# A graph-attention layer: the first difference of W_v by an adding transfer, query loads on GpSimd, and other tiles turned by VectorE

## The chip, the cores and the metric

The kernel runs on one core of a Trainium2 chip. The metric is the device time of one execution in microseconds (us). The engines are named as the profile names them: PE is TensorE, DVE is VectorE, ACT is ScalarE, POOL is GpSimd, SP is SyncE. Each has one instruction queue that it works off in order. PE's weight loads (PEld) run beside its matmuls. Transfers are issued by SP, ACT or POOL and carried out by sixteen DMA engines.

## The reference

One layer over 2708 nodes with 1024 features, all in float32:

```python
h = jnp.maximum(_layernorm(x, axis=-1), 0.0)
q = h @ W_q.T + b_q
k = h @ W_k.T + b_k
v = h @ W_v.T + b_v
z = scale * (q @ k.T)
spare_z = z * adj_tensor
spare_z = jnp.where(spare_z == 0.0, -10000.0, spare_z)
attn = jax.nn.softmax(spare_z, axis=1)
return x + jax.nn.relu(attn @ v)
```

The adjacency matrix is random with about 0.15% ones, some four per row.

## The kernel before

**What is computed.** W_q and W_k are folded into one matrix M, so that a score is the product of a row of q = h M + b with a row of h. Since a row has few neighbours, no 2708 x 2708 product is formed: the rows are sorted by degree into 22 tiles of 128 rows (P), and for each tile and each neighbour slot POOL gathers the neighbours' rows of h by an indirect transfer (`gather`, L610). DVE multiplies a gathered tile g with the tile's queries pq and sums along the row (L863, one score for each row), and after the softmax adds the gathered tiles up with their weights into u (L923, L929 for a half tile). The output is relu(u W_v + b) + x.

**The two large products.** Both h M and u W_v are done for pairs of tiles in a Strassen-Winograd scheme: seven products of blocks in place of eight. Its sums of blocks of the weights are T0 = W01 − W00, T1 = W11 − T0, T2 = W11 − W01 and T3 = W10 − T1 (subtractions in L1270 on DVE, in `T`, which the profile calls `wlow`); its sums of blocks of the rows are named s1 to s4 (`blocks`, L711 to L742, DVE). There are 20 units: 0 to 9 make q for a pair of tiles, 10 to 19 make the output of the pairs (6,5), (4,3), (2,0), (20,7), (17,13), (18,12), (19,11), (15,10), (14,1) and (16,9). Tile 8 has no partner: it comes alone, in four plain products behind unit 19 (L1372 to L1380). One product is four matmul instructions of 128x512 over 128x128 (L1011, eight rows of the profile). In PE's queue the seven of a unit stand so: s2, a12, s4, s3, then two of the next unit (a11, s1, issued by `opened`), then a22.

**Order.** The places between a unit's products are numbered: `after(i)` with i from 0 to 6 is called behind each, and the code there says what is issued at (unit, i). DVE's queue is in the order in which the program names its instructions. Those of PE, ACT, POOL and SP are placed by a scheduler as their inputs become ready in its model. The attention is a stream of steps, advanced by `advance` by a share of time at each `after`, over tiles in the order 6, 5, 4, 3, 2, 21, 0, 20, 7, 17, 13, 18, 12, 19, 11, 15, 10, 14, 1, 16, 9, 8. Tile 21 is a second half for rows of high degree. `fill` issues gathers as slots come free: `free` holds the slots, and pieces of the weight buffers join it once their weights are used. `fetch` gets a tile's queries pq: tiles 0 to 7 by a POOL gather, the others from `q_late` by a plain SP load (L833; L831 for the half tile 21). There are two pq buffers.

**Turning u.** A product needs u with features on the partitions. Three ways are used. A *faced* tile goes through DRAM: ACT copies it permuted (L945) and stores it (L947), SP loads it in four pieces (`by_quarters`, L700), and DVE turns it in 32x32 blocks (`faces`, L705, STREAM_TRANSPOSE). Any other tile is turned by PE, in eight matmuls with the identity (`half_turned`, L415), and ACT copies from PSUM (L718). A tile whose unit is near (`near`) is held in SBUF for it, without the trip. L940 decides which tiles are faced, by the place `now` at which the tile is done. Before, these are all tiles of the first five output units, and tile 8, whose rows are loaded at the end of unit 18 and turned by DVE behind the first product of unit 19 (`T_alone`). PE turns 18, 12, 19, 11, 15, 10, 14, 1, 16 and 9.

**The weights.** M's place is taken by W_v block by block as M's last products are done (L1263 to L1266, SP). W01 comes first, asked for at 219.26 us into M[:, 0, 1], which the products of M do not read. T0 is made at (9, 2).

Of the kernel before, what the change touches and what calls it, by code (L numbers as in the profile page):

```python
# [18 lines left out]
P = 128  # L19
# [46 lines left out]
def tile_preln_masked_attention(  # L66
# [753 lines left out]
    def fetch(t):  # L820

        if t not in g_of:
            ask(t)
        if t == BARE:
            return
        assert formed.issuperset(range(EARLY) if t < EARLY or t == SECOND else (t,)), t
        tq[t] = work.tile([P, D], FT, tag="hT", name=f"pq_{t}", bufs=2)
        if t == SECOND:
            assert EARLY in formed
            gather(tq[t][:HP], q_dram[:, :], t, SLOTS - WIDE, HP)  # L830
            nc.sync.dma_start(tq[t][HP:], q_late[:HP, :])  # L831
        elif t >= EARLY:
            nc.sync.dma_start(tq[t], q_late[(t - EARLY) * P:(t - EARLY + 1) * P, :])  # L833
        else:
            got = gather(tq[t], q_dram[:, :], t, SLOTS, P)
            if t == order[0]:
                first_q.append(got)
# [81 lines left out]
    def sums(t):  # L919
# [19 lines left out]
        unit = next((n for n, pair in enumerate(units) if pair[0] == "o" and t in pair[1:]), len(units))  # L939
        if now < [unit - 2, 2] and unit <= len(q_pairs) + 4 or unit >= len(units) - 1:  # L940
            faced_tiles.add(t)
# [74 lines left out]
    def opened(n):  # L1016
# [7 lines left out]
        nc.scalar.copy(Y, X)  # L1024
        products.append(add_block(Z, ops["s1"], T[:, 0]))
        p5 = small("p5")
# [203 lines left out]
    for n, unit in enumerate(units):  # L1230
# [13 lines left out]
        def after(i):  # L1244
# [13 lines left out]
            if n == FIRST and i in (1, 4, 5):  # L1258
                for g in slots[:4] if i == 1 else slots[4:6] if i == 4 else slots[6:8]:
                    with tc.issue_after(sorted_at[-1].ins):  # L1260
                        nc.vector.memset(g, 0.0)
            b11, b12, b21, b22 = M[:, 0, 0], M[:, 0, 1], M[:, 1, 0], M[:, 1, 1]
            for at, place, src in (((-1, 0), b12, of_wv(0, 1)), ((0, 0), b11, of_wv(0, 0)), ((0, 2), T[:, 1], of_wv(1, 1)),  # L1263
                                   ((0, 3), b21, of_wv(1, 0)), ((0, 4), b22, of_wv(1, 1))):
                if (n - last_q, i) == at:
                    nc.sync.dma_start(place, src)  # L1266
            for at, place, a, b in (((0, 2), T[:, 0], b12, b11), ((0, 4), T[:, 1], T[:, 1], T[:, 0]),
                                    ((1, 0), T[:, 2], b22, b12), ((1, 1), T[:, 3], b21, T[:, 1])):
                if (n - last_q, i) == at:
                    nc.vector.tensor_sub(place, a, b)  # L1270
            if (n - last_q, i) == (1, 1):
                free.extend(M.rearrange("p i j (a c) w -> p i j a (c w)", a=2)[:, 0, 1, a, :] for a in range(2))
            if (n, i) == (FIRST, 5):
# [11 lines left out]
            if nxt is not None:  # L1285
# [12 lines left out]
                if i == 6 and n + 2 < FIRST:  # L1298
                    natural_rows(n + 2)
                if i == (2 if n in (FIRST, last_q) else 4) and n + 2 > FIRST and n + 2 < len(units) and n + 2 not in rows_of:  # L1300
                    while units[n + 2][0] == "o" and not done.issuperset(units[n + 2][1:]):
# [13 lines left out]
            if nxt is None and i == 1:  # L1315
                uT = work.tile([P, D], FT, tag="hT", name="T_alone", bufs=2).rearrange("p (c q) -> p c q", q=P)
                faces(uT, single["rows"], 0, DC)
                single["turned"] = uT
            if n == len(units) - 2 and i == 6:
                while alone not in done:  # L1320
                    advance(1.0)
                single["rows"], = load_rows(("o", alone))
            if nxt is None and i == 3:
# [48 lines left out]
    uT, (X, Z), p1 = single["turned"], single["banks"], single["first"]  # L1372
    add_block(Z, uT[:, 0:4, :], T[:, 0])
    add_block(Z, uT[:, 4:8, :], M[:, 1, 1])
# [188 lines left out]
```

## Time and profile before

| | us |
|---|---|
| three runs | 637.52, 638.18, 638.37; median 638.18 |
| the profiled execution | 638.0, of which its span 636.3 |
| granted clock of PE, mean | 0.995 |
| PE busy | 624.6 |
| DVE busy | 525.7 |
| POOL busy | 361.8 |
| ACT busy | 283.5 |

Up to about 120 us the kernel folds the matrices and reads the adjacency matrix; the q units follow, and the output units from about 390 us on. Behind the last matmul there are some 9 us of the last DVE sum, its POOL scatter and the transfer. In the lines quoted below, a timeline's row has the start, the duration, the engine, the line of the kernel, the operation, output<-input, and in brackets how long the engine was idle before it and what it waited for. A row of groups ends with busy time and mean duration in ns. A row of the waits has the engine and its tile or line, what it waited for, then us in total, times and the longest. A row of the windows has the length, then busy time and instructions of PE, PEld, DVE, ACT and POOL, the granted clock, the share of the DMA engines and GB/s.

### The profile page before, as it was taken

The page shows a single profiled execution, that of the slowest core. Times are in us where ns is not written, and L with a number is a line of the kernel's source. Part 1 is how long each engine was busy: PE and PEld are TensorE (multiplying, and loading weights), DVE is VectorE, ACT ScalarE, POOL GpSimd, SP SyncE. Part 2 cuts the span into 40 slices and gives each one's busy share as a digit, 9 for nine tenths or more (in the row PEclk, how much of TensorE's full clock was granted, in tenths as well). Part 3 has the DMA queues.
Part 4 walks back from the last instruction along what each step waited for, and adds up shares of the span by engine and source line. Part 5 has one row for each costly group of instructions (what it writes and reads, how often), then busy time and mean ns, then how long its engine had stood idle before and what let it go on. Part 6 is the DMA issues. An engine that isn't in the chain of part 4 may idle for free.

```text
span 636.3 us, 6139 instructions
## 1 busy us (share of the span) xinstructions
PE 624.6 (98%) x1627; PEld 315.5 (50%) x1627; DVE 525.7 (83%) x1021; ACT 283.5 (45%) x421; POOL 361.8 (57%) x383
## 2 busy tenths in 40 slices
PE   9999999999999999999999999999999999999994
PEld 5777766444444544444444434444444444444441
DVE  5999889897995755997889999999999989898341
ACT  3539975859667533424341243443343333422300
POOL 2649960975868277563742563576566777632431
PEclk9999999999999999999999999999999999999997
DMA  8998897598696439986699998999999999893761
GB/s 339 407 372 310 334 351 298 199 342 328 246 382 221 170 113 334 326 299 196 194 289 323 297 412 216 311 318 324 351 378 321 334 299 295 242 289 95 210 217 40
DMA packets 62352, 180.11 MB, mean 283 GB/s; under 512 B 10039, under 2 KB 17031, under 8 KB 61672
## 3 DMA queue, kind: packets, MB, share of 16 engines
q0 software_dynamic: 25136, 78.41, 39.4%
q1 hardware_dynamic: 31242, 80.19, 35.8%
q10 hardware_dynamic: 5934, 21.06, 8.5%
q8 instruction: 15, 0.25, 0.2%
q14 instruction: 25, 0.20, 0.1%
HBM read 147.23 MB, written 42.31 MB: 298 GB/s over the span
## 4 chain that ended last, share of the span: by engine, by line
PE 85%; DVE 6%; issue 4%; DMA 3%; SPq 1%; POOL 0%; ACT 0%; POOLq 0%; DVEq 0%; ACTq 0%
PE ps L1011 38%; PE psy L1011 28%; PE ps_y L476 6%; PE ps_x L476 4%; PE ps_z L476 4%; PE pt L415 3%; DVE u L923 2%; DMA g<-h_dram,tab 1%; DMA or<-u_dram 1%; DVE junk L863 1%; DVE s L722 1%; DVE wlow L1270 1%; PE ps_y L511 1%; SPq L700 1%; DVE q L1092 0%
## 5 line engine op out<-in xcount | busy, mean ns | idle before, releaser
L610 POOL DMA_INDIRECT g<-h_dram,tab x94 | 121.4, 1291 | 84.4 <-DVE u L923 31.1
L1011 PE MATMUL ps<-M,a 128*128 128x512 f32 x320 | 144.0, 593 | 0.0
L1011 PE MATMUL psy<-wlow,s 128*128 128x512 f32 x320 | 143.9, 592 | 0.0
L863 DVE SCALAR_TENSOR_TENSOR junk<-g,pq 128x1024 uint8<-128x1024 f32 x93 | 113.7, 1222 | 14.0 <-DMA g<-h_dram,tab 10.9
L1011 PEld LDWEIGHTS ps<-M,a 128*128 128x128 f32 x320 | 59.8, 190 | 70.8 <-issue 70.6
L1011 PEld LDWEIGHTS psy<-wlow,s 128*128 128x128 f32 x320 | 59.7, 190 | 70.2 <-issue 69.4
L923 DVE SCALAR_TENSOR_TENSOR u<-g,coef,u 128x1024 f32<-128x1024 f32 x69 | 88.4, 1281 | 6.9 <-ACT u L912 5.8
L389 DVE FIND_INDEX8 at<-ones,adj 128x8 uint32<-128x685 f32 (+1 forms) x88 | 74.5, 865 | 0.0
L1011 PE MATMUL psy<-wlow,a 128*128 128x512 f32 x160 | 72.0, 593 | 1.4 <-DVE q L1092 1.4
L1011 PE MATMUL ps<-M,s 128*128 128x512 f32 x160 | 72.1, 592 | 0.0
L1011 PE MATMUL ps<-wlow,s 128*128 128x512 f32 x160 | 72.0, 593 | 0.1
L368 ACT ACTIVATE sized<-adj 128x2708 uint8<-128x2708 f32 (+1 forms) x22 | 54.3, 2468 | 7.5 <-DMA adj<-in_adj_dram 6.2
L298 POOL TENSOR_TENSOR hsum<-hsum,x 128x256 f32<-128x256 f32 (+1 forms) x56 | 38.7, 729 | 25.6 <-DVE wlow L444 21.2
L1110 POOL DMA_INDIRECT y<-in_x_dram,tab x19 | 34.8, 1832 | 29.1 <-ACT y L1127 15.9
L1011 PEld LDWEIGHTS psy<-wlow,a 128*128 128x128 f32 x160 | 30.3, 190 | 40.0 <-issue 37.1
L1011 PEld LDWEIGHTS ps<-wlow,s 128*128 128x128 f32 x160 | 30.3, 190 | 38.6 <-issue 37.9
L1011 PEld LDWEIGHTS ps<-M,s 128*128 128x128 f32 x160 | 30.3, 190 | 38.1 <-issue 37.4
L912 ACT ACTIVATE u<-g,coef 128x1024 f32<-128x1024 f32 x18 | 20.7, 1147 | 32.1 <-DVE coef L911 32.1
L808 POOL DMA_INDIRECT out_dram<-y,tab x21 | 25.0, 1188 | 16.4 <-DVE flag L1354 6.1
L626 POOL DMA_INDIRECT tab_dram<-tab,pos_i x22 | 21.9, 995 | 20.7 <-DVE pos_i L689 15.3
L276 ACT ACTIVATE x<-x,r 128x1024 f32<-128x1024 f32 (+1 forms) x22 | 25.9, 1235 | 7.3 <-POOL r L266 7.3
L760 ACT COPY ps<-bp_sb 128x512 f32<-128x512 f32 x42 | 24.5, 595 | 7.2 <-DVE y L1145 6.7
(251 smaller groups left out, 843.5 us busy)
## 6 DMA issues: line engine op xcount, KB each, us to landing
adj<-in_adj_dram SPq DMA_DIRECT2D x21, 1354.0 KB, 11.3
x<-in_x_dram SPq DMA_DIRECT2D x21, 512.0 KB, 3.9
h_dram<-x ACTq DMA_DIRECT2D x21, 512.0 KB, 8.7
u_dram<-v ACTq DMA_DIRECT2D x13, 512.0 KB, 6.4
or<-u_dram SPq DMA_DIRECT2D x52, 128.0 KB, 7.0
q_late<-q SPq DMA_DIRECT2D x12, 512.0 KB, 6.0
pq<-q_late SPq DMA_DIRECT2D x12, 512.0 KB, 8.6
M<-in_wv_dram SPq DMA_DIRECT2D x4, 1024.0 KB
```

The lines of the kernel that those rows point to most:

```text
L276: nc.scalar.activation(xs[i][:n], xs[i][:n], AF.Relu, bias=r[:n, 4, i:i + 1], scale=r[:n, 3, i:i + 1])
L298: small.append(nc.gpsimd.tensor_add(hsum[:n, cols], hsum[:n, cols], xt[:n, cols]))
L368: nc.scalar.activation(sized[:n], a[:n, :, :PW], AF.Abs, accum_out=total[:n, t:t + 1])
L389: nc.vector.max_index(at[:n, k - first_k, g, :], ones[:n, 0:8], a[:n, g, :])
L476: mm = nc.tensor.matmul(bank, a_tile(o + H * a[0], a[1], i), b(o), start=first and o == 0, stop=(o == H - 1), skip_group_check=True)
L610: return nc.gpsimd.indirect_dma_start(out=dst, out_offset=None, in_=src, in_offset=off, bounds_check=N - 1, oob_is_err=False)
L760: nc.scalar.copy(return_[h], row[:, h * NB:(h + 1) * NB])
L808: to = nc.gpsimd.indirect_dma_start(out=out, out_offset=bass.IndirectOffsetOnAxis(ap=ptab.bitcast(U32)[:n, t, SLOTS:SLOTS + 1], axis=0), i ...
L863: chained(lambda: nc.vector.scalar_tensor_tensor(junk, g_of[t][s], 1.0, tq[t], op0=ALU.mult, op1=ALU.mult, accum_out=zall[:, t, s:s + 1]))
L923: chained(lambda: nc.vector.scalar_tensor_tensor(u, g_of[t][s], coef[:, s:s + 1], u, op0=ALU.mult, op1=ALU.add))
L1011: mm = nc.tensor.matmul(bank, a[:, c, :], b[:, c, :], start=False, stop=(c == 3), skip_group_check=True)
L1110: return nc.gpsimd.indirect_dma_start(out=y[:n], out_offset=None, in_=x, in_offset=off, compute_op=ALU.add)
```

## The change

- **First difference.** W00 is loaded into M[:, 0, 1], at SP's place where W01 was loaded before. ACT scales it by −1 in place in two instructions, and a POOL transfer with `accum_op=add` adds W01 from DRAM to it: T0 stands there without DVE. T0's subtraction goes; T2 is now formed as T1 − W00. The s1 products of the output units and of tile 8 read M[:, 0, 1], and T[:, 0] joins the gather slots at (9, 0), where two pieces of M[:, 0, 1] joined at (10, 1) before.
- **Queries.** The twelve L833 loads and L831 go from SP's queue to POOL's.
- **Faced tiles.** By the new condition 18, 12 and 19 are faced. Tile 8 no longer is: it is held, turned by PE ahead of unit 19's s2 product, and copied by ACT. Tile 15 is now held too.
- **Rows sooner.** From unit 9 on the rows of unit n + 2 are loaded at i = 2 and not at i = 4 where both tiles are done.

```diff
@@ fetch
             gather(tq[t][:HP], q_dram[:, :], t, SLOTS - WIDE, HP)
-            nc.sync.dma_start(tq[t][HP:], q_late[:HP, :])
+            nc.gpsimd.dma_start(tq[t][HP:], q_late[:HP, :])
         elif t >= EARLY:
-            nc.sync.dma_start(tq[t], q_late[(t - EARLY) * P:(t - EARLY + 1) * P, :])
+            nc.gpsimd.dma_start(tq[t], q_late[(t - EARLY) * P:(t - EARLY + 1) * P, :])
@@ sums
-        if now < [unit - 2, 2] and unit <= len(q_pairs) + 4 or unit >= len(units) - 1:
+        if now < [unit - 2, 1] and unit <= len(q_pairs) + 6 or unit == len(units) - 1:
             faced_tiles.add(t)
@@ opened
-        products.append(add_block(Z, ops["s1"], T[:, 0]))
+        products.append(add_block(Z, ops["s1"], T[:, 0] if units[n][0] == "q" else M[:, 0, 1]))
@@ after
-            b11, b12, b21, b22 = M[:, 0, 0], M[:, 0, 1], M[:, 1, 0], M[:, 1, 1]
-            for at, place, src in (((-1, 0), b12, of_wv(0, 1)), ((0, 0), b11, of_wv(0, 0)), ((0, 2), T[:, 1], of_wv(1, 1)),
+            b11, t1, b21, b22 = M[:, 0, 0], M[:, 0, 1], M[:, 1, 0], M[:, 1, 1]
+            for at, place, src in (((-2, 0), t1, of_wv(0, 0)), ((0, 0), b11, of_wv(0, 0)), ((0, 2), T[:, 1], of_wv(1, 1)),
                                    ((0, 3), b21, of_wv(1, 0)), ((0, 4), b22, of_wv(1, 1))):
                 if (n - last_q, i) == at:
                     nc.sync.dma_start(place, src)
-            for at, place, a, b in (((0, 2), T[:, 0], b12, b11), ((0, 4), T[:, 1], T[:, 1], T[:, 0]),
-                                    ((1, 0), T[:, 2], b22, b12), ((1, 1), T[:, 3], b21, T[:, 1])):
+            if (n - last_q, i) == (-2, 6):
+                for h in range(2):
+                    nc.scalar.activation(t1[:, 2 * h:2 * h + 2], t1[:, 2 * h:2 * h + 2], AF.Copy, scale=-1.0)
+                nc.gpsimd.dma_start(t1, of_wv(0, 1), accum_op=ALU.add)
+            for at, place, a, b in (((0, 4), T[:, 1], T[:, 1], t1), ((1, 0), T[:, 2], T[:, 1], b11),
+                                    ((1, 1), T[:, 3], b21, T[:, 1])):
                 if (n - last_q, i) == at:
                     nc.vector.tensor_sub(place, a, b)
-            if (n - last_q, i) == (1, 1):
-                free.extend(M.rearrange("p i j (a c) w -> p i j a (c w)", a=2)[:, 0, 1, a, :] for a in range(2))
+            if (n - last_q, i) == (0, 0):
+                free.extend(T.rearrange("p k (a c) w -> p k a (c w)", a=2)[:, 0, a, :] for a in range(2))
...
-                if i == (2 if n in (FIRST, last_q) else 4) and n + 2 > FIRST and n + 2 < len(units) and n + 2 not in rows_of:
+                ready = n >= last_q and n + 2 < len(units) and done.issuperset(units[n + 2][1:])
+                if (i == 4 or i == 2 and (n == FIRST or ready)) and n + 2 > FIRST and n + 2 < len(units) and n + 2 not in rows_of:
...
             if nxt is None and i == 1:
-                uT = work.tile([P, D], FT, tag="hT", name="T_alone", bufs=2).rearrange("p (c q) -> p c q", q=P)
-                faces(uT, single["rows"], 0, DC)
-                single["turned"] = uT
-            if n == len(units) - 2 and i == 6:
                 while alone not in done:
                     advance(1.0)
-                single["rows"], = load_rows(("o", alone))
+                r, = load_rows(("o", alone))
+                single["turned"] = turned(r, "alone")
@@ behind the units
-    add_block(Z, uT[:, 0:4, :], T[:, 0])
+    add_block(Z, uT[:, 0:4, :], M[:, 0, 1])
```

The change moves instructions at three places. The first is DVE's queue in unit 9, where `q` is the last pair's queries, `or` a faced tile's rows and `s`, `a` its blocks. Before:

```order
L1329 TENSOR_TENSOR bp_sb<-bp_sb 128x512
L1270 TENSOR_TENSOR wlow<-M 128x2048
L923 SCALAR_TENSOR_TENSOR u_2292<-g_1412,coef,u_2292 128x1024
L705 STREAM_TRANSPOSE a_2319<-or_2235 128x4x4x32
L705 STREAM_TRANSPOSE s_2321<-or_2235 128x4x4x32
...
L1095 TENSOR_TENSOR q_2272<-ps_2218,u_2314 128x512
L1270 TENSOR_TENSOR wlow<-wlow 128x2048
```

and now:

```order
L1331 TENSOR_TENSOR bp_sb<-bp_sb 128x512
L923 SCALAR_TENSOR_TENSOR u_2295<-g_1412,coef,u_2295 128x1024
L705 STREAM_TRANSPOSE a_2321<-or_2238 128x4x4x32
L705 STREAM_TRANSPOSE s_2323<-or_2238 128x4x4x32
...
L1095 TENSOR_TENSOR q_2275<-ps_2221,u_2317 128x512
L1274 TENSOR_TENSOR wlow<-wlow,M 128x2048
```

T0's subtraction is gone from between the bias and the weighted sum; T1's (now L1274) stays, and reads M[:, 0, 1].

The second is POOL's queue in the middle of the output units: `g`, `M` and `wlow` are gather slots, `y` the rows of x that are added, `out_dram` the scatter of a finished tile. Before:

```order
L1110 DMA y_2706<-in_x_dram,tab 128x1024
L808 DMA out_dram<-y_2562,tab 2708x1024
L610 DMA g_1403<-h_dram,tab 128x1024
L610 DMA g_1404<-h_dram,tab 128x1024
L610 DMA g_1405<-h_dram,tab 128x1024
L1110 DMA y_2841<-in_x_dram,tab 128x1024
L808 DMA out_dram<-y_2705,tab 2708x1024
L610 DMA g_1406<-h_dram,tab 128x1024
```

and now, with the names numbered by tile:

```order
L1110 DMA y_0_2708<-in_x_dram,tab_97 128x1024
L808 DMA out_0_dram<-y_3_2564,tab_97 2708x1024
L833 DMA pq_10_2977<-q_late_65 128x1024
L610 DMA g9_1412<-h_dram_63,tab_97 128x1024
L610 DMA g10_1413<-h_dram_63,tab_97 128x1024
L610 DMA g0_1403<-h_dram_63,tab_97 128x1024
L1110 DMA y_20_2847<-in_x_dram,tab_97 128x1024
L808 DMA out_0_dram<-y_2_2707,tab_97 2708x1024
L833 DMA pq_14_3082<-q_late_65 128x1024
L610 DMA g1_1404<-h_dram_63,tab_97 128x1024
```

A plain load of queries now stands ahead of the gathers, once for each tile. Likewise the half tile's load and the adding transfer have come into POOL's queue; the latter stands between a gather and two loads of rows for the q units:

```order
L610 DMA g_1412<-h_dram,tab 128x1024
L610 DMA g_1413<-h_dram,tab 128x1024
L1270 DMA M<-in_wv_dram 128x2048
L612 DMA qr_1737<-h_dram,tab 128x1024
L612 DMA qr_1739<-h_dram,tab 128x1024
```

The third is PE's queue at the end. Before, from the last two products that unit 18's place holds to the single tile:

```order
L1011 MATMUL ps_3655<-M,a_3611 128x512 x4
L1011 MATMUL ps_3657<-wlow,s_3641 128x512 x4
L1011 MATMUL psy<-wlow,a_3519 128x512 x4
L1011 MATMUL psy<-wlow,s_3644 128x512 x4
L1011 MATMUL ps_3655<-M,a_3613 128x512 x4
```

and now:

```order
L1011 MATMUL ps_3640<-M,a_3596 128x512 x4
L1011 MATMUL ps_3642<-M,s_3626 128x512 x4
L1011 MATMUL psy<-wlow,a_3504 128x512 x4
L415 MATMUL pt<-ident,u_3606 128x128 x8
L1011 MATMUL psy<-wlow,s_3629 128x512 x4
L1011 MATMUL ps_3640<-M,a_3598 128x512 x4
```

Tile 8's eight transposes (`u_3606`) stand between unit 18's last product and unit 19's first; everything to the end is behind them. The three groups of eight on `or` for tiles 18, 12 and 19 are gone from the middle of the queue.

## The prediction

> **What bounds the kernel now.** I read the page's busy times first, then what TensorE (PE) waits for, then what VectorE (DVE) waits for in the second half, then the timelines of the places that the change touches.
>
> ```profile
> PE 624.6 (98%) x1627; PEld 315.5 (50%) x1627; DVE 525.7 (83%) x1021; ACT 283.5 (45%) x421; POOL 361.8 (57%) x383
> ...
> PE 85%; DVE 6%; issue 4%; DMA 3%; SPq 1%; POOL 0%; ACT 0%; POOLq 0%; DVEq 0%; ACTq 0%
> ...
> PE psy L1011 <- DVE q L1092: 1.4, 1, 1.4
> ```
>
> PE is busy for 98% of the span, and in the second half the one wait listed for it is 1.4 us. So a change can win only what it takes out of PE's own queue: that stall, or PE instructions. The stall, with what DVE did before it:
>
> ```profile
> 352.79 2.28 DVE L1270 TENSOR_TENSOR wlow<-M 128x2048 f32<-128x2048 f32 x1
> ...
> 363.37 2.28 DVE L1270 TENSOR_TENSOR wlow<-wlow 128x2048 f32<-128x2048 f32 x1
> ...
> 368.08 0.68 DVE L1092 TENSOR_TENSOR q<-psy,p 128x512 f32<-128x512 f32 x1
> ...
> 363.81 3.60 PE L1011 MATMUL ps<-wlow,s 128*128 128x512 f32 x8
> 368.81 3.70 PE L1011 MATMUL psy<-wlow,a 128*128 128x512 f32 x8 [1.41 <-DVE q L1092]
> 372.35 3.60 PE L1011 MATMUL psy<-wlow,s 128*128 128x512 f32 x8
> 375.79 3.60 PE L1011 MATMUL ps<-M,a 128*128 128x512 f32 x8
> ```
>
> Two blocks of matmuls start 3.44 apart when PE waits for nothing (372.35 to 375.79), and 5.00 apart here: 1.56 us are lost, because DVE reaches L1092 late in an order written by hand, with both first L1270 subtractions ahead of it.
>
> DVE is the second bound. Over the output units it is busy in 255.8 of 275 us, and it waits for gathers and for ACT, never for PE:
>
> ```profile
> 462.00:514.00 52.00, 52.00 (x147) 24.78 (x146) 48.05 (x77) 19.80 (x35) 37.99 (x29) 1.00 1.01 343
> ...
> sum 275.00, PE 273.53 PEld 125.67 DVE 255.79 ACT 94.22 POOL 159.44; mean PE 54.71 PEld 25.13 DVE 51.16 ACT 18.84 POOL 31.89
> ...
> DVE junk L863 <- DMA M<-h_dram,tab: 1.8, 1, 1.8
> DVE junk L863 <- DMA g<-h_dram,tab: 1.8, 2, 1.0
> DVE p L1122 <- ACT taken L1076: 1.2, 2, 1.0
> DVE s L722 <- ACT a L718: 1.0, 1, 1.0
> DVE a L705 <- DMA or<-u_dram: 0.5, 1, 0.5
> ```
>
> So DVE's attention runs at its own pace, and what matters is when its last sum, that of the single tile 8, is done, and who needs it. Before, there is room: the turned tile comes from a round trip through DRAM and DVE waits 11.56 us for it. The end of DVE's stream and the PE blocks at that time:
>
> ```profile
> 591.14 1.27 DVE L929 SCALAR_TENSOR_TENSOR u<-g,m,u 64x1024 f32<-64x1024 f32 x1
> ...
> 605.03 1.25 DVE L705 STREAM_TRANSPOSE T_alone<-or 128x1024 f32<-128x1024 f32 x1 [11.56 <-DMA or<-u_dram]
> ...
> 592.52 3.60 PE L1011 MATMUL psy<-wlow,a 128*128 128x512 f32 x8
> 595.95 3.60 PE L1011 MATMUL psy<-wlow,s 128*128 128x512 f32 x8
> ```
>
> **Removed from PE.** Tiles 18, 12 and 19 are no longer turned by PE: three groups of eight L415 transposes.
>
> ```profile
> 468.78 1.04 PE L415 MATMUL pt<-ident,or 128*128 128x128 f32 x8
> 469.65 3.60 PE L1011 MATMUL psy<-wlow,s 128*128 128x512 f32 x8
> ```
>
> A group holds the next block up by 0.87 (469.65 − 468.78), so −2.61. Added: one such group for tile 8, +0.87.
>
> **First difference of W_v.** T0's subtraction at 352.79 goes: DVE −2.28, ahead of L1092. Its place is taken by two in-place ACT scalings by −1 and one adding transfer, long before the first output unit needs it. The new ACT pair stands between these two rows:
>
> ```profile
> 226.76 0.62 ACT L760 COPY ps<-bp_sb 128x512 f32<-128x512 f32 x1
> 231.69 0.59 ACT L1076 COPY taken<-psy 128x512 f32<-128x512 f32 x1 [4.31 <-PE psy L1011]
> ...
> L375 ACT ACTIVATE junk_m<-M x8: 1057/1064/1082, 205.8 to 224.2; 128x1024 uint8<-128x1024 f32 x8
> ```
>
> Two ACTIVATEs over 128x1024 at 1.06 are 2.1 us in a gap of 4.31: nothing, if W00 has landed by 227.4. It is asked for by SyncE at 219.26, as W01 was before; the DMA row over 217 to 262 in forty slices of 1.125 us is empty from the eighth slice (224.9) on, so it has:
>
> ```profile
> DMA  5629881000001890787998887989999999999878
> ```
>
> The cover gone, ACT would be late for L1076 and PE with it, by what is missing; that price is bounded by the gap, 4.31, and I take 0. The further megabyte flows among the gathers at 250 to 290; it is as much as two gathers of 512 KB, which POOL issues 1.3 apart (1.01 + 0.30, the row at 286.32 below): 0 to 2.6 of later gathers. DVE catches up with PE behind them:
>
> ```profile
> 279.82 0.69 DVE L1095 TENSOR_TENSOR q<-ps,u 128x512 f32<-128x512 f32 x1 [0.52 <-PE ps L1011]
> ```
>
> Up to 0.5 of a delay ends in this wait; I take 0 for the transfer and leave the 2.1 above it to the range.
>
> **The second half-tile's load on POOL.** L831 now stands between two gathers for which DVE waits:
>
> ```profile
> 284.10 1.91 POOL L610 DMA_INDIRECT g<-h_dram,tab  x1 [0.30 <-DVE q L1092]
> 286.32 1.01 POOL L610 DMA_INDIRECT g<-h_dram,tab  x1 [0.30 <-issue]
> ...
> 295.85 1.23 DVE L863 SCALAR_TENSOR_TENSOR junk<-g,pq 128x1024 uint8<-128x1024 f32 x1 [0.94 <-DMA g<-h_dram,tab]
> ...
> 344.21 0.57 POOL L845 DMA_DIRECT2D g<-v_dram  x1 [5.24 <-DMA v_dram<-u]
> 353.48 2.46 POOL L610 DMA_INDIRECT g<-h_dram,tab  x1 [0.30 <-issue]
> 380.23 3.00 POOL L610 DMA_INDIRECT g<-h_dram,tab  x1 [0.30 <-DVE a L705]
> ```
>
> The only direct load on POOL, L845, took 0.57, and 0.30 lies between two issues: 0.9 each. The upper bound is the slowest gather, 3.0 + 0.3. I take 0.9, the same kind of transfer. DVE is then 0.9 later from 295 on, and L1092 gains 2.28 − 0.9 = 1.38 of the 1.56 lost (0 to 1.56): PE −1.4.
>
> **Twelve more loads on POOL.** SyncE's queue (SPq) holds 1% of the chain above, so their leaving it wins nothing. On POOL most have cover. Four of them (tiles 10, 14, 16, 9) fall into the stretch where POOL issues back to back and DVE waits for its gathers:
>
> ```profile
> 469.59 1.02 POOL L610 DMA_INDIRECT g<-h_dram,tab  x1 [0.30 <-issue]
> ...
> 480.77 1.23 DVE L863 SCALAR_TENSOR_TENSOR junk<-g,pq 128x1024 uint8<-128x1024 f32 x1 [0.82 <-DMA g<-h_dram,tab]
> ...
> 500.99 1.23 DVE L863 SCALAR_TENSOR_TENSOR junk<-g,pq 128x1024 uint8<-128x1024 f32 x1 [0.96 <-DMA g<-h_dram,tab]
> ...
> 523.78 1.22 DVE L863 SCALAR_TENSOR_TENSOR junk<-M,pq 128x1024 uint8<-128x1024 f32 x1 [1.83 <-DMA M<-h_dram,tab]
> ```
>
> 4 x 0.9 = 3.6 later gathers, against some 2.9 that DVE itself is later there (next part): +0.7 is left. Bounds: −3.6 (the three waits vanish behind the longer DVE work) and 4 x 3.3 − 2.9 = +10.3.
>
> The Trainium skill ("SBUF — State Buffer", "Who interferes with whom") says that a transfer issued by GpSimd can be starved by VectorE through a shared port pair and that one issued by another engine can't, which speaks against this move. The row of 3.00 us beside DVE work agrees for gathers, which read a table; L845's 0.57 does not show it for direct loads. By the stretched row the sum would be that of the fourth case below.
>
> **Three more tiles on DVE.** A faced tile costs DVE its L705 transposes; the subtractions stay.
>
> ```profile
> L705 DVE STREAM_TRANSPOSE a<-or 128x512 f32<-128x512 f32 x12 | 8.0, 693 | 0.5 <-DMA or<-u_dram 0.5
> L705 DVE STREAM_TRANSPOSE s<-or 128x512 f32<-128x512 f32 x4 | 2.7, 668 | 0.0
> ```
>
> Sixteen transposes for four pairs, 10.7 us: 1.34 a tile, +4.0 for three. What leaves DVE: the wait for ACT's copy of a PE-turned tile (1.0), the wait for rows, loaded earlier now (0.5), and the waits for ACT's L1076 (1.2), which a later DVE finds done. The stretch is so 4.0 − 1.0 = about 3 later, less at first: the 2.9 above.
>
> **The single tile.** PE's eight transposes of tile 8 stand directly ahead of the block that started at 595.95, and behind them on PE is everything to the end. They need DVE's L929, which ended at 592.41. PE gets there at 595.95 − 1.4 − 2.61 = 591.94. The 1.25 us of DVE at 605 were in its idle time and win nothing. Call the shift of L929 by everything above D:
>
> D = 0.9 (L831) − 2.28 (T0) + 4.0 (faced) − 1.0 − 0.5 − 1.2 + 0.7 (gathers) = +0.6.
>
> The block then starts at 592.41 + 0.6 + 0.05 (L1092 ended 0.05 ahead of its block at 368.81) + 0.87 = 593.93, 2.0 earlier than before, and the rest follows as it was. Taken from the profiled execution, 638.0 (span 636.3 and 1.7 around it), that is 636.0; the median, 638.18, is a little above it: 636.1.
>
> **The rivals.**
> *PE's own queue decides* (D under −0.5): the gather waits of 3.6 vanish in the longer DVE work, and PE saves 1.4 + 2.61 − 0.87 = 3.1: 634.9. For it: those waits are short; against: DVE has only about 4 idle us in 52.
> *It cancels* (D from 1.3 to 3.9): the time that T0 leaves is spent waiting, for rows of an earlier tile or a weight block still on its way, so that −2.28 is not had: D = 2.9, block at 596.2, gain −0.3: 638.4. The change then moves PE's work and saves none. An ACT pair held up by a late W00 ends here too.
> *Slower: POOL's queue stretches.* Each of the four loads in the back-to-back stretch takes 2 us or more, as gathers beside DVE work do, and each gather behind it lands as much later: 4 x 2 − 2.9 = 5.1 in place of 0.7, D = 5.0, the single tile's transposes hold PE until 596.9 and the block starts at 598.3: 2.4 lost, 640.5. It decides as soon as D passes 2.6, where the room of 2.6 us that PE has is used up. For it: the 3.00 row, and the slack of the gathers there is next to none; against: 0.57 at L845.
>
> **How the numbers follow.** Forecast (D from −0.5 to 1.3) 0.42, PE's queue 0.2, cancelled 0.21, slower 0.17. About 0.2%, 1.3 us, is what a measurement of this kernel tells from no change, so faster is under 636.9: 0.42 + 0.2 = 0.62; same 0.21; slower 0.17. The forecast's own range is 635.3 to 637.0; with PE's queue below and the milder half of the slower case above, 634.5 to 639.4.
>
> **What would show it.** L1092's wait gone or under 0.3; no L415 between 465 and 500 on `or`; an L415 group just ahead of unit 19's s2 block with a wait for DVE L929 of some 1 us; ACT's L1076 near 231 unmoved; L833 on POOL at 0.5 to 0.7; DVE's gather waits between 462 and 531 not above 4.5 in sum. A load of 2 us and more on POOL, a wait of PE for L929 of over 3 us, or a new wait of PE between 400 and 590 makes it wrong.

## The result, and the profile after

The changed kernel is slower. Its median is 640.53 us (638.44 to 643.1, 12 runs) against 638.0 of the kernel before in the same session: a ratio of 1.0042, 95% interval 1.003 to 1.0053. In a second session it was 1.0031 (1.0012 to 1.0049). The forecast was 636.1, faster, with 634.5 to 639.4 as its range.

The profiled execution took 639.78 (span 638.1), one of the faster of the twelve. The page's busy times and the chain that ended last:

```profile
PE 623.4 (98%) x1611; PEld 313.6 (49%) x1611; DVE 526.3 (82%) x1025; ACT 287.1 (45%) x422; POOL 371.6 (58%) x397
...
PE 83%; DMA 10%; DVE 4%; issue 1%; ACT 0%; SPq 0%; POOL 0%; POOLq 0%; DVEq 0%
```

PE is busy for 1.2 us less, with sixteen matmul records fewer (two groups of transposes). Transfers have become a tenth of the chain, some 62 us, where they were 3%; 26 us of it are two blocks of W_v, shown below, and most of the rest lies before 202 us. PE's waits:

```profile
PE ps L1011 <- DMA M<-in_wv_dram: 2.0, 1, 2.0
PE ps_y L511 <- POOL hsum L121: 1.2, 1, 1.2
PE pt L415 <- DVE u L929: 0.7, 1, 0.7
PE ps L1011 <- DVE s L722: 0.5, 1, 0.5
PE pt L415 <- DMA qr<-h_dram,tab: 0.4, 1, 0.4
```

The wait for L1092 is gone, as forecast. A wait for a block of W_v has come, and the one for tile 8 (L929). PE's timeline where the first output unit begins:

```profile
368.62 3.60 PE L1011 MATMUL psy<-wlow,a 128*128 128x512 f32 x8
372.05 3.60 PE L1011 MATMUL psy<-wlow,s 128*128 128x512 f32 x8
377.68 3.70 PE L1011 MATMUL ps<-M,a 128*128 128x512 f32 x8 [2.03 <-DMA M<-in_wv_dram]
381.45 3.67 PE L1011 MATMUL ps<-M,s 128*128 128x512 f32 x8
```

From 372.05 to 377.68 are 5.63 and not 3.44: the a12 product waits 2.2 for W10. Subtracting the starts of like products in the two profiles gives an account of the profiled execution, up to its end:

| PE's place | before | after | after − before | what came in |
|---|---|---|---|---|
| unit 3, behind a transpose of rows | 201.26 | 202.64 | +1.38 | 0.06 from the start on; DVE's L722 late, +0.73; a gather of rows late, +0.59 |
| a22 product that waited for L1092 | 368.81 | 368.62 | −0.19 | that wait, −1.57 |
| a12 product of unit 10 | 375.79 | 377.68 | +1.89 | W10, +2.19 (and −0.11 in the product before it) |
| s2 product of unit 15 | 469.65 | 470.79 | +1.14 | one group of transposes less, −0.87; small gaps, +0.12 |
| s2 product of unit 19 | 595.95 | 597.07 | +1.12 | two groups less; tile 8's and its wait, +1.74 |
| last scatter issued by POOL | 628.24 | 629.37 | +1.13 | |
| end of the span | 636.3 | 638.1 | +1.8 | the last scatter, issue to end: 8.06, then 8.73 |

The first row does not belong to the change: the second profile of the same kernel has this product at 201.73, without either wait, and over the profiles of all kernels it lies between 201.21 and 204.66. Without this row PE's last products would start 0.3 sooner than before; the span would still be 0.4 longer, since the last scatter took 0.7 more to end. (It took 8.2 to 8.9 in the other profiles, so the 8.06 of the profile before is the shortest of all.) The stall that came is larger than the one that was won (2.1 against 1.6), and most of what the transposes gave goes at tile 8. Most executions of the changed kernel are longer than the profiled one; this is taken up below.

Why W10 is late, in SP's queue (before, then after), in POOL's (after) and in the chain that ended last (after):

```profile
350.95 3.78 SPq L700 DMA_DIRECT2D or<-u_dram  x7
357.23 0.92 SPq L1266 DMA_DIRECT2D M<-in_wv_dram  x2
```

```profile
352.03 5.16 SPq L700 DMA_DIRECT2D or<-u_dram  x7
360.22 2.21 SPq L1266 DMA_DIRECT2D M<-in_wv_dram  x2
```

```profile
346.36 1.85 POOL L610 DMA_INDIRECT wlow<-h_dram,tab  x1 [0.30 <-issue]
348.52 2.00 POOL L610 DMA_INDIRECT wlow<-h_dram,tab  x1 [0.31 <-PE psy L1011]
...
356.83 0.57 POOL L833 DMA_DIRECT2D pq<-q_late  x1 [0.78 <-DMA q_late<-q]
```

```profile
351.65 8.51 DMA wlow<-in_wv_dram
360.16 0.02 issue
360.18 0.02 SPq L1266
360.19 0.03 issue
360.22 17.42 DMA M<-in_wv_dram
```

The two `wlow` gathers go into T[:, 0], free from (9, 0) on by the change; the kernel before made the like of them at 376.90 and 378.94. With these ahead, seven loads of rows take SP 5.16 and not 3.78. They are done at 357.19 all the same, and W10 is issued only at 360.22: by the chain, SP waits 3.0 there for the block loaded ahead of it (W11, into `wlow`) to land. That took 8.5 us. In the kernel before SP waits 2.4 at this place for the same transfer, which was issued at 350.27; from its issue to W10's are 6.96 there and 8.57 here.

W10 is issued 11.83 ahead of unit 10's s2 product (372.05 − 360.22) where it was 15.12 (357.23 against 372.35). Of these 3.29, 1.61 are the slower W11, and 1.68 come from PE, which no longer stalls at L1092 and so is at s2 that much sooner behind W11's issue: the stall that was won takes the slack of the next load. W10 itself then needs 17.4 us to land.

DVE's waits in the output units (389.5 to 600):

```profile
DVE p L1122 <- ACT taken L1076: 4.7, 3, 2.0
DVE u L923 <- ACT u L912: 2.9, 2, 1.6
DVE u L1126 <- PE ps L1011: 2.1, 2, 1.1
DVE s L722 <- ACT a L718: 0.3, 1, 0.3
```

No wait for a gather is left in this stretch, so POOL's queue does not delay DVE there. In their place DVE, held to its written order, waits 6.8 us for PE's products (L1122 through ACT's copy, L1126), and tile 8 is late in turn (DVE, then PE):

```profile
594.76 1.27 DVE L929 SCALAR_TENSOR_TENSOR u<-wlow,m,u 64x1024 f32<-64x1024 f32 x1
```

```profile
591.90 3.60 PE L1011 MATMUL psy<-wlow,a 128*128 128x512 f32 x8
596.17 1.06 PE L415 MATMUL pt<-ident,u 128*128 128x128 f32 x8 [0.67 <-DVE u L929]
```

The edits whose price was disputed, by groups of instructions:

```profile
L833 POOL DMA_DIRECT2D pq<-q_late x12 | 7.6, 633 | 18.9 <-DVE junk L863 18.1 <-DMA q_late<-q 0.8
L1269 ACT ACTIVATE M<-M 128x1024 f32<-128x1024 f32 x2 | 2.0, 1073 | 0.0
L831 POOL DMA_DIRECT2D pq<-q_late x1 | 0.6, 596 | 0.0
```

A load of queries takes POOL 0.63 in the mean (eleven take 0.57 to 0.60, one 1.17), the two scalings ACT 2.0.

One correction to the description of the kernel above: tiles 16 and 9 are faced before and after, and PE does not turn them. Nothing in the argument rests on them.

### The profile page after: what moved, and what is told of

Read it like the earlier page. It is cut to its first block, busy times and chain, and to the rows that moved or that the text cites. A ratio compares the mean times of both kernels' runs of the same rounds, so it can differ in the third digit from the quotient of the medians.

```text
span 638.1 us, 6111 instructions
## 1 busy us (share of the span) xinstructions
PE 623.4 (98%) x1611; PEld 313.6 (49%) x1611; DVE 526.3 (82%) x1025; ACT 287.1 (45%) x422; POOL 371.6 (58%) x397
## 4 chain that ended last, share of the span: by engine, by line
PE 83%; DMA 10%; DVE 4%; issue 1%; ACT 0%; SPq 0%; POOL 0%; POOLq 0%; DVEq 0%
PE ps L1011 37%; PE psy L1011 27%; PE ps_y L476 6%; PE ps_x L476 4%; PE ps_z L476 4%; PE pt L415 3%; DMA M<-in_wv_dram 3%; DMA adj<-in_adj_dram 2%; DMA h_dram<-x 2%; DMA wlow<-in_wv_dram 1%; DMA qr<-h_dram,tab 1%; DMA or<-u_dram 1%; PE ps_y L511 1%; DVE u L923 1%; DVE st L237 1%
## 5 line engine op out<-in xcount | busy, mean ns | idle before, releaser
L610 POOL DMA_INDIRECT g<-h_dram,tab x94 | 117.6, 1251 | 54.9 <-issue 18.0
L1011 PE MATMUL ps<-M,a 128*128 128x512 f32 x320 | 144.1, 593 | 2.0 <-DMA M<-in_wv_dram 2.0
L1011 PE MATMUL psy<-wlow,s 128*128 128x512 f32 x320 | 143.9, 592 | 0.0
L1011 PE MATMUL ps<-M,s 128*128 128x512 f32 x240 | 108.0, 592 | 0.1
L1011 PEld LDWEIGHTS ps<-M,a 128*128 128x128 f32 x320 | 59.8, 190 | 73.7 <-issue 70.2
L923 DVE SCALAR_TENSOR_TENSOR u<-g,coef,u 128x1024 f32<-128x1024 f32 x70 | 89.7, 1281 | 7.1 <-ACT u L912 5.8
L1011 PEld LDWEIGHTS psy<-wlow,s 128*128 128x128 f32 x320 | 59.8, 190 | 70.5 <-issue 68.2
L1011 PEld LDWEIGHTS ps<-M,s 128*128 128x128 f32 x240 | 45.4, 190 | 57.6 <-issue 56.9
L1011 PE MATMUL psy<-wlow,a 128*128 128x512 f32 x160 | 71.9, 592 | 0.0
L1011 PEld LDWEIGHTS psy<-wlow,a 128*128 128x128 f32 x160 | 30.4, 190 | 38.3 <-issue 37.8
L808 POOL DMA_INDIRECT out_dram<-y,tab x21 | 27.8, 1322 | 16.8 <-DMA y<-in_x_dram,tab 7.6
L1011 PE MATMUL ps<-wlow,s 128*128 128x512 f32 x80 | 36.0, 593 | 0.5 <-DVE s L722 0.5
L626 POOL DMA_INDIRECT tab_dram<-tab,pos_i x22 | 21.9, 993 | 19.9 <-DVE pos_i L689 14.4
L945 ACT COPY v<-u 128x1024 f32<-128x1024 f32 x15 | 15.7, 1046 | 36.9 <-DVE u L923 32.6
L912 ACT ACTIVATE u<-g,coef 128x1024 f32<-128x1024 f32 x17 | 19.5, 1148 | 22.1 <-DVE coef L911 17.1
L476 PE MATMUL ps_y<-wlow 128*128 128x512 f32 x64 | 27.6, 592 | 0.0
## 6 DMA issues: line engine op xcount, KB each, us to landing
M<-in_wv_dram SPq DMA_DIRECT2D x4, 1024.0 KB, 14.4
```

The source lines that it names most:

```text
L476: mm = nc.tensor.matmul(bank, a_tile(o + H * a[0], a[1], i), b(o), start=first and o == 0, stop=(o == H - 1), skip_group_check=True)
L610: return nc.gpsimd.indirect_dma_start(out=dst, out_offset=None, in_=src, in_offset=off, bounds_check=N - 1, oob_is_err=False)
L626: put = nc.gpsimd.indirect_dma_start(out=tab_dram[lo >= EARLY][:, :], out_offset=bass.IndirectOffsetOnAxis(ap=pos_i[:n, t:t + 1], axis=0), ...
L808: to = nc.gpsimd.indirect_dma_start(out=out, out_offset=bass.IndirectOffsetOnAxis(ap=ptab.bitcast(U32)[:n, t, SLOTS:SLOTS + 1], axis=0), i ...
L923: chained(lambda: nc.vector.scalar_tensor_tensor(u, g_of[t][s], coef[:, s:s + 1], u, op0=ALU.mult, op1=ALU.add))
L1011: mm = nc.tensor.matmul(bank, a[:, c, :], b[:, c, :], start=False, stop=(c == 3), skip_group_check=True)
```

## The experiments

Ratios are to the kernel before, run on the same chip in turns with it; medians of different sessions are not compared.

| run | what it is | median, us | before, us | ratio (95% interval) |
|---|---|---|---|---|
| e1_sp | after, queries on SP | 645.07 | 637.84 | 1.0098 (1.0064 to 1.0131) |
| e2_slots | after, slots late | 637.03 | 637.84 | 0.9996 (0.9981 to 1.001) |
| e3_faced | after, 18, 12, 19 on PE | 639.42 | 637.84 | 1.0034 (1.0014 to 1.0055) |
| e4_single | after, tile 8 on VectorE | 638.49 | 637.84 | 1.0023 (1.0006 to 1.0041) |
| e6_later | e2, tile 8 one product later | 638.59 | 640.9 | 0.9976 (0.9956 to 0.9996) |
| b1_diff | before, first difference, slots late | 641.72 | 640.9 | 1.0008 (0.9989 to 1.0027) |
| e7_w10 | after, W10 issued by ACT | 642.46 | 640.9 | 1.0025 (0.9996 to 1.0054) |
| b2_pool | before, queries on POOL | 643.48 | 640.9 | 1.003 (0.9994 to 1.0066) |
| r_after | after once more | 639.35 | 638.03 | 1.0031 (1.0012 to 1.0049) |
| r_later | e6 once more | 635.46 | 638.03 | 0.9965 (0.9953 to 0.9978) |
| e8_sp | e6, queries on SP | 639.5 | 638.03 | 1.0017 (0.9997 to 1.0036) |
| b3_both | b1, queries on POOL | 636.87 | 638.03 | 0.9983 (0.9974 to 0.9992) |

**Slots late.** The edit, shortened:

```diff
-            if (n - last_q, i) == (0, 0):
-                free.extend(T.rearrange(...)[:, 0, a, :] for a in range(2))
+            if (n - last_q, i) == (1, 1):
+                late.extend(T.rearrange(...)[:, 0, a, :] for a in range(2))
+                free.extend(late)
@@ fill: the first gather into each of the two
-                with tc.issue_after(first_q[0].ins) if first_q else nullcontext():
+                with tc.issue_after(gathered[-1].ins if first_use else first_q[0].ins) if first_q else nullcontext():
```

> The changed kernel with T[:, 0] as gather slots only from (10, 1) on, and its first two gathers behind the gather that precedes them in the program, so that they are issued near 376 as in the kernel before. Theory A: two thirds of what came ahead of W10 is gone; the wait near 378 is under 0.5, DVE's waits for PE's products (L1122, L1126, 6.8 us together) shrink to under 4, and the time is 638.0 to 638.8. Rival B: 640.5, wait unchanged. Rival C: 640.5, PE's wait for L929 unchanged at 0.7.

637.03 against 637.84 of the kernel before: this one part takes back what the change lost (0.9981 to 1.001, against 1.003 to 1.0053 and 1.0012 to 1.0049 of the changed kernel). The gain that was forecast, 636.1 / 638.18 = 0.997, is not had even so. The wait for W10 is gone. In SP's queue and PE's:

```profile
351.32 3.96 SPq L700 DMA_DIRECT2D or<-u_dram  x7
357.62 1.01 SPq L1271 DMA_DIRECT2D M<-in_wv_dram  x2
```

```profile
371.34 3.60 PE L1016 MATMUL psy<-wlow,s 128*128 128x512 f32 x8
374.77 3.60 PE L1016 MATMUL ps<-M,a 128*128 128x512 f32 x8
...
588.59 3.60 PE L1016 MATMUL psy<-wlow,a 128*128 128x512 f32 x8
593.58 1.06 PE L415 MATMUL pt<-ident,u 128*128 128x128 f32 x8 [1.39 <-DVE u L934]
594.48 3.60 PE L1016 MATMUL psy<-wlow,s 128*128 128x512 f32 x8
```

(Added lines shift this kernel's numbers by five: L1016 is L1011, L934 is L929, L1271 is L1266.) W10 goes out 13.72 ahead of s2, and a12 follows s2 after 3.43. W11 landed after 6.6 us and W10 after 14.2, where they took 8.5 and 17.4. What is left on PE's path is 1.39 for tile 8. DVE's waits at the counterparts of L1122 and L1126 are 4.2 where under 4 was expected, and the time is below the expected 638.0 to 638.8.

**Queries back on SP.**

```diff
-            nc.gpsimd.dma_start(tq[t], q_late[(t - EARLY) * P:(t - EARLY + 1) * P, :])
+            nc.sync.dma_start(tq[t], q_late[(t - EARLY) * P:(t - EARLY + 1) * P, :])
```

and likewise L831.

> The changed kernel with L831 and the twelve L833 loads back on SP's queue, all else as changed. Theory A (a weight block comes late): PE's wait for W10 near 378 (2.0 us) has 1.5 MB more ahead of it than before: two gathers into T[:, 0] at 346 and 349 and tile 17's queries at 357. With the query load behind the weights again, a third of that is gone: the wait falls to 1.0 or below, the time to about 639.5. Rival B (POOL's queue): the loads on POOL delay the gathers and so DVE; then the time goes to 638 or below, with the wait at 378 still near 2. Rival C (DVE's own work on three more faced tiles, and PE's wait for tile 8): no change, 640.5.

Theory A has the wait right, which is gone; the time, 645.07, is far from all three. DVE's and PE's timelines of this kernel:

```profile
384.52 1.23 DVE L863 SCALAR_TENSOR_TENSOR junk<-wlow,pq 128x1024 uint8<-128x1024 f32 x1 [5.50 <-DMA pq<-q_late]
```

```profile
391.99 5.37 PE L1011 MATMUL ps<-M,s 128*128 128x512 f32 x8 [3.43 <-DVE s L722]
```

Without T0's subtraction DVE comes to tile 17's first score sooner. On SP that tile's queries stand behind two stores of q, which wait for the last q tiles, and go out at 372.47 (POOL: 356.83). DVE comes to that score 3.3 sooner than before (379.02 against 382.29) and waits 5.5, so the queries also came at least 2.2 later than before, though they were asked for 1.4 sooner (372.47 against 373.84). PE waits 3.43 for DVE's sums, and its next block takes 5.37 and not 3.60: from 392 to 396 its granted clock was 0.57. So the move to POOL is no loss; with the first difference it is needed.

The profile also bears on W10. The two early gathers are there, W10 goes out 12.97 ahead of s2, and PE does not wait for it: with the query load of 356.83 gone from ahead of W10, the early gathers alone did not make it late in this execution.

**The first difference alone**, made from the kernel before, with late slots:

> The kernel before with the first difference alone (two ACT scalings, the adding transfer, T[:, 0] as slots only near 376); queries on SP, faced tiles and tile 8 as before. Theory: the adding transfer costs nothing and PE's stall at L1092 (1.56) goes, but DVE, 2.28 earlier, finds tile 17's queries not there (they are behind stores on SP, at 373.8): a wait of DVE for pq of 1 to 3 us near 380, and 636.5 to 638. Rival 1: the adding transfer is what costs (ACT late at 231 or gathers late): over 638.5. Rival 2: the stall goes and no wait comes for it: under 636.5.

The kernel before took 640.9 beside this run, so that the times expected can't be used and the ratio must do: 1.0008, no gain. The stall at L1092 is gone but for 0.2 (the a22 product starts 3.65 behind the one before it), and the wait for queries is there:

```profile
386.56 1.23 DVE L868 SCALAR_TENSOR_TENSOR junk<-g,pq 128x1024 uint8<-128x1024 f32 x1 [3.16 <-DMA pq<-q_late]
```

The profiled execution is the slowest of its twelve, 645.41: behind this wait PE waited 3.01, and its next block took 6.69.

**Queries on POOL alone**, made from the kernel before:

> The kernel before with the thirteen loads of queries on POOL and nothing else. Theory: DVE never waits for queries in the kernel before, so moving them wins and loses nothing beyond their issue on POOL, 0.9 each in the stretch where POOL is dense: 637.5 to 639. Rival (my fourth case, POOL's queue stretches): loads of 2 us and more, later gathers, 640 or above.

1.003, with an interval that holds no change: on its own the move wins nothing. Its twelve loads took 0.57 to 0.62, so the rival's stretched loads did not come.

**Both together.**

> The kernel of b1 (first difference alone, late slots) with the queries on POOL as well. Theory: each of the two parts alone wins nothing, together they do, since the wait for pq near 386 is gone and PE's stall at L1092 too: 0.2 to 0.5% below the kernel before, with no wait for pq. Rival: same time as b1.

0.9983, and every one of its eleven runs lies between 636.58 and 637.48. PE has no wait behind unit 3, and nothing is listed for `pq`. Two edits, of which neither showed a gain alone, win 0.17% together; slightly less than the 0.2 expected. The interval (0.9974 to 0.9992) just meets that of b1 (0.9989 to 1.0027), which was run on another chip, so that this pair of runs leans to the theory and does not prove it; e8 below, beside e6's kernel in one session, is the stronger one.

**Tiles 18, 12 and 19 on PE again.**

```diff
-        if now < [unit - 2, 1] and unit <= len(q_pairs) + 6 or unit == len(units) - 1:
+        if now < [unit - 2, 2] and unit <= len(q_pairs) + 4 or unit == len(units) - 1:
```

> The changed kernel with tiles 18, 12 and 19 turned by PE again (tile 8 as changed). Rival C: DVE has 4.0 us less to do, L929 ends some 2 to 4 earlier and PE's wait for it is gone: 638 to 639. Theory A: the wait for W10 stays at 2.0; PE has 2.6 more of transposes and loses only the 0.7 wait: 641.5 to 642.5. Rival B: 640.5 to 642.

639.42, between the two. In its profile, an execution of 638.11, W10 came in time (issued 14.17 ahead of s2) and PE waits for nothing but the fold at the start, so the wait for L929 is gone as rival C had it. The run does not tell the theories apart; it shows that W10's wait is not in every execution, though the early slots were there.

**Tile 8 on VectorE again.** Its code as before the change, with M[:, 0, 1] in its second product.

> The changed kernel with tile 8 faced and turned by VectorE again (three more faced tiles as changed). PE loses the eight transposes and the wait for L929, 0.87 + 0.67. Theory A: the W10 wait stays, and the round trip of tile 8 through DRAM, 12.6 us behind L929 before, ends just about when its first product is due: 639.0 to 640. Rival C (the single tile on PE is what costs): 638.5 or below. Rival B: 639 to 640.

638.49, under the 639 to 640 of theories A and B and just within what rival C (the single tile on PE is what costs) expected, 638.5 or below. The ratio, 1.0023 (1.0006 to 1.0041), can't be told from that of the changed kernel, so the time decides nothing. The wait for W10 is there as theory A had it, and the round trip comes late:

```profile
PE ps L1011 <- DMA M<-in_wv_dram: 2.4, 2, 2.0
...
PE ps L1011 <- DVE T_alone L705: 1.1, 1, 1.1
```

**W10 issued by ACT.**

```diff
-                    nc.sync.dma_start(place, src)
+                    (nc.scalar if at == (0, 3) else nc.sync).dma_start(place, src)
```

> The changed kernel with W10's load issued by ACT and not by SP, where it stood behind seven loads of rows that took SP 5.2 us and came out at 360.2 (357.2 before). If SP's hold-up is the cause of PE's wait near 378, W10 lands 3 earlier and the wait is gone: 638 to 639. If the bytes ahead of it are (the transfers were busy all the time from 345 on), the wait stays at 1 to 2: 640 to 641.

ACT issued it at 358.81, 17.0 ahead of the s2 product and 3.4 behind W11's issue, and a12 followed s2 without a wait, though the two gathers stood ahead of it as in the changed kernel. Issued sooner, W10 is in time; whether SP's row loads or its wait for W11 is what holds W10 up, this run does not separate. But the next product then waited 1.35 for ACT's L760, and the time, 1.0025 with an interval from 0.9996, decides nothing. That a load at another place mends it is not shown.

**Tile 8 one product later**, on top of late slots.

```diff
-            if nxt is None and i == 1:
+            if nxt is None and i == 2:
                 while alone not in done:
```

> The kernel of e2 with tile 8's eight transposes one product later (at i = 2, behind unit 19's s2 block). In e2 PE waited 1.4 us for L929's counterpart there, the last wait on its path. Theory: PE arrives 3.4 later, the wait is gone and 1.4 come off: 635.4 to 636.0, faster than both kernels. Rival: PE's path is held by something else by then (ACT's two copies, T_alone late for its first product), then 636.5 to 637.5.

0.9976, against 0.9996 with the transposes a product sooner, on another chip and with intervals that overlap. Its profile shows what else lengthened it:

```profile
203.38 1.25 PE L415 MATMUL pt<-ident,qr 128*128 128x128 f32 x8 [2.10 <-DMA qr<-h_dram,tab]
204.42 5.14 PE L1016 MATMUL psy<-wlow,s 128*128 128x512 f32 x8
```

The gather near 202 was 2.10 late, and the block behind it took 5.14 and not 3.60; from 204 to 208 the granted clock was 0.57. The profile of e7 shows the like (2.46, then 5.29); b1 and b2 waited there too (2.37 and 1.73), without a slow block behind it. Run once more, beside the changed kernel:

> The kernel of e6 once more, beside the changed kernel on one chip: no wait of PE behind 210 us but the early ones of 0 to 2.5 that all kernels show; 0.994 to 0.998 of the kernel before and 0.7 to 1.0% below the changed one.

0.9965 (0.9953 to 0.9978, so below e2's interval), its five runs between 635.3 and 636.47. PE's timeline at the end:

```profile
591.80 3.60 PE L1016 MATMUL psy<-wlow,s 128*128 128x512 f32 x8
595.24 1.04 PE L415 MATMUL pt<-ident,u 128*128 128x128 f32 x8
596.11 3.60 PE L1016 MATMUL ps<-M,a 128*128 128x512 f32 x8
```

The transposes cost 0.87 and no wait. PE's like products are 3.28 sooner than before at the end (599.39 to 596.11). This is the version that beats both kernels: 635.46 against 638.03 and 639.35 of the changed one, which is 0.61% more (639.35 / 635.46), where 0.7 to 1.0 was expected. Its median as a time misses what was expected of e6 in the first session, whose chip ran all kernels longer (638.59 beside 640.9), and meets it in the second.

**The changed kernel once more.**

> The changed kernel once more, for a second profile of it. Theory A (W10 comes late, by an amount that differs from execution to execution): PE waits for a weight block or, behind it, DVE for PE's products; the time stands 0.3 to 0.6% over the kernel before. If the first profile's 2.0 was chance, no such wait shows and the ratio is 1.000 to 1.002.

```profile
PE ps L1011 <- DMA M<-in_wv_dram: 1.8, 1, 1.8
...
PE pt L415 <- DVE u L929: 0.8, 1, 0.8
```

The same two waits. Its twelve runs go from 637.6 to 645.58.

**Queries on SP, in the kernel of e6.**

> The kernel of e6 with the loads of queries back on SP. Theory: without T0's subtraction DVE comes to tile 17's first score 2 us sooner than before, and on SP its queries stand behind two stores that wait for the last q tiles: DVE waits 2 to 6 us for pq near 384, PE 2 to 4 for L722 near 392, and the time is 0.5 to 1.0% above that of e6. Rival (leaving SP wins nothing, as predicted): within 0.2% of e6.

1.0017 against 0.9965 of the same kernel with the queries on POOL, half a per cent, in one session: the rival falls. DVE waits 5.4 for `pq` in all, in two waits, and the largest is 2.8. PE's wait for L722 is smaller than expected (1.8 in two) and others for ACT have come (2.9 in two).

## Why the prediction was wrong

**The step that failed** is the one on the first difference, with "I take 0 for the transfer and leave the 2.1 above it to the range". It weighed the scalings and the transfer, and left out what the edit also moves: T[:, 0] becomes free at (9, 0), and the next two gathers go there, 30 us sooner. They had to be counted as transfers that pass others. W11, issued behind them, lands after 8.5 and not 6.6 (e2); SP issues W10 only then; W10 takes 17.4 and not 14.2; and PE, which by the won stall is there sooner, loses 2.2. With the gathers at their old place the wait is gone, and the loss of time with it (e2). The three profiles with the wait (after, r_after, e4) have W10 issued 11.8 to 12.0 ahead of s2 and landed after 17.1 to 17.5; those of e1, e3 and e7 have the gathers early, W10 issued 13.0 to 17.0 ahead, and no wait. The cancelling case did name "a weight block still on its way", but as a wait of DVE and a price of zero in sum.

Of the 3.8 us by which the profiled execution lies above the 636.0 worked out for it, W10 is 2.1, 1.4 came before 203 us and 0.7 in the last scatter, neither of them shown to be the change's; the rest of the path comes out 0.4 better than forecast. So the 2.1 is a loss that the forecast had no place for, and the size of the miss in that one execution is in part chance.

**The second step that failed** is "so their leaving it wins nothing" on the twelve loads. SP's share of the chain told of the kernel before, whose DVE came to tile 17's queries late enough not to wait. The edit beside it takes 2.28 out of DVE, and then these loads are what it waits for when they stay on SP: 3.16 in b1, 5.5 in e1. This did not make the changed kernel slower, since the loads had left SP; it hid that the move was what the first difference needed. The parts were priced one by one against the old timeline. They depend on each other: with the first difference in place the move is worth half a per cent (e8 against r_later), and on its own nothing that b2 could show.

**Right in mechanism and size.** The wait for L1092 went (−1.57; −1.4 forecast). The three groups of transposes took 2.63 out of PE (0.87, 0.88 and 0.88 in the shifts; 2.61 forecast). ACT's two scalings fitted into the gap (2.0; L1076 still waited 2.40 for PE). The loads on POOL took 0.63 in the mean and 0.30 between issues, so 0.93 against 0.9. None of the signs that the prediction named as making it wrong appeared: PE's new wait was at 376, and it had looked for one between 400 and 590.

**Right in mechanism, wrong in size.** Tile 8 is what PE waits for at the end. L929 ended 3.6 later than before and not 0.6 (596.03 against 592.41), 1.4 of it from what came before 203. With W10 in time, in e2, its counterpart ended 1.0 later (593.43), near the forecast. Of the sum, "− 1.2" for the waits behind L1076 had the wrong sign: they grew, with those for PE, from 1.2 to 6.8. W10 is a part of that and not all: with W10 in time these waits are still 4.2 in e2, 5.3 in r_later and 5.6 in b3. A DVE that no longer waits for gathers comes to PE's products before they are done; this is argued from the waits and not shown by a run. The gather waits went altogether (−3.6), where +0.7 was taken.

**The rivals.** The slower case had the time (640.5) and not the cause, which is luck. (Its "until 596.9" should be 597.5, from L929 at 592.41 + 5.0; the 598.3 behind it is right.) Its loads of 2 us on POOL did not come: 0.57 to 0.60 each, one of 1.17. The Trainium skill's rule on transfers issued by GpSimd beside VectorE ("SBUF — State Buffer", "Who interferes with whom") is so not seen here for plain loads.

**What stays open.** The profiled executions of the changed kernel, 639.78 and 638.34, are among its faster ones, and show 2.0 and 1.8 for W10. Its others reach 643 and more. That W10 is later still in those is likely, since the two kernels with late slots and queries on POOL that have five and eleven runs in the last session spread over 1.2 and 0.9 us, the changed one over 8. Against it, e8 has late slots too, with queries on SP, and spreads over 7. The granted clock says more: nine of the changed kernel's 24 executions have a mean of 0.993 or less, all nine at 640.0 us or above, and none of the kernel before's 54 on that chip in the sessions of experiments. In the four profiles with such a mean (e1, e6, e7, b1) PE waited for 2.10 us or more at one place, and the block behind it ran 1.5 to 3.1 us longer than the 3.60 of the others. So a wait only slightly longer than the 2.03 seen for W10 may cost as much again and more. Which wait it is in the nine is not shown: none of the changed kernel's executions over 640 was profiled. e2, with the same late slots, has one run of 640.47 and one of 639.17 among eleven, so late slots are not all of it, and on the chip of e6 every kernel spread by 5 us and more, with the gather near 202 late in all four profiles. Whether the two early gathers make W10 late without the query load of 356.83 beside them, the one profile of e1 can't settle. The earlier loads of rows (at i = 2) and the holding of tile 15 were not run by themselves.

## What to carry to other kernels

When an edit frees a buffer sooner, ask which transfers then go sooner, and which load that the bound engine needs is issued behind them: the bytes are the same, but the order is not. Price an edit against the timeline that the other edits leave, since an engine made 2 us earlier meets waits that the old profile cannot show. And where an in-order engine must take a late result, put that work one step later if its own reader has the time; with that, the 1.4 us for which PE had waited in e2 were gone in r_later. A load that has just enough time is also at risk when an earlier stall is won, since the engine then comes to it sooner.

## What the runs showed of the hardware

Seven row loads of 128 KB took SP 3.56 to 4.03 us to issue in the eight profiles where the two gathers of 512 KB stood late, and 4.06 to 7.28 in the six where they were issued 3.5 to 7.3 us ahead. A weight block of 1 MB issued next to them landed after 8.4 to 8.6 us in the three of these profiles with the wait, and after 5.4 to 6.6 in four with late gathers (e2, r_later, e8, b3); the next one, 17.1 to 17.5 against 12.1 to 14.4. The adding transfer of 1 MB took POOL 1.02 to issue, as much as a gather of 512 KB, and no wait for its result was seen.

A longer wait of PE cost more than itself. Of the waits above 2.03 us, 2.10, 2.46, 3.01 and 3.43 (e6, e7, b1, e1) had a block of products behind them that took 5.14, 5.29, 6.69 and 5.37 and not 3.60, with a granted clock of 0.50 to 0.66 over the next 4 us; 2.37 and 2.44 (b1 and e1, at other places) had none. Behind the waits of 2.03 and less, in the same profiles and the others, the next block took 3.60 to 3.70.
